# A graph layer on one core: three banks for tiles' products, batch sums in one go, evictions in turn

## The chip, the core and the metric

The kernel runs on one core of a Trainium2 chip. A core has a matrix engine (TensorE, PE in the profile; its weight loads are shown as PEld), a vector engine (VectorE, DVE), a scalar engine (ScalarE, ACT), GpSimd (POOL) and a sync engine (SP) that issues transfers. Each engine runs its own list of instructions in order and waits on semaphores for the others. TensorE writes its products to PSUM, which has eight banks of 2 KiB per partition here, and VectorE and ScalarE read them from there. The metric is the time of one execution on the device in microseconds (us), lower is better. The time before is 18,458.98 us, the median of three runs (18,452.1 to 18,463.75).

## What is computed

Two layers of a relational graph network over 50,000 nodes with 128 features, 850,000 edges sorted by destination and 16 relations, then a residual and a layer norm. Cut to its core:

```python
def _rgcn_layer(h, src, dst, rel, basis, w_comp, loop_w, bias):
    W = jnp.einsum('rb,bio->rio', w_comp, basis)          # 16 relations from 8 bases
    seg = dst.astype(jnp.int32) * N_REL + rel.astype(jnp.int32)
    agg = jax.ops.segment_sum(h[src], seg, num_segments=N_ENT * N_REL)
    agg = agg.reshape(N_ENT, N_REL, -1)
    msg = jnp.einsum('nri,rio->no', agg, W)
    out = msg + h @ loop_w + bias
    return jax.nn.relu(out)

h = _rgcn_layer(x, src, dst, rel_type, basis1, w_comp1, loop_w1, bias1)
h = _rgcn_layer(h, src, dst, rel_type, basis2, w_comp2, loop_w2, bias2)
x = _layernorm(x + h, axis=-1)
```

Everything is float32.

## The kernel before

**Chunks and tiles.** 50,000 of the edges lead from a node to itself and are treated apart (below). The other 800,000 are cut into 625 chunks of ten tiles of 128 edges, and every layer goes over all 625 (`for c in range(C)`, inside `for n, of in enumerate((x, H1))`), 1,250 chunks in all. A tile's edges reach few nodes, 12 at most (`WN`), so a tile is summed into 12 slots, for each of 8 bases.

**Gathers.** For each tile GpSimd issues one indirect transfer (`gather`, L202) that fetches the 128 source rows into `rows[buffer][:, k, :]`. There are five buffers of ten tiles; chunk c+2's gathers are written in the program at chunk c, and a gather waits until the matmul that last read its place is done.

**Tiles' products.** VectorE makes for each chunk a matrix `hot` (`hot_of`, L869 and L876) that holds, for each edge, its weight for each of the 8 bases at the slot of its destination. TensorE multiplies each tile's rows with its part of `hot` (L974, 128 x 96 out). Five tiles, half a chunk, share one PSUM bank `pa` of the pool `ps_a`, which has two. In the text below "product" is one such matmul; it leaves two records in the trace, as the other matmuls of full size do. When a bank has its five products, ScalarE copies it to `aT` in SBUF (L982). `aT` holds four chunks, one batch: 8 bases x 480 slots.

**Batch sums.** When a batch is complete, `slots_of_batch` (L742) multiplies it with the eight basis matrices, summed over them in one bank `ps` (L746), the only bank of the pool `ps_s`; ScalarE copies that to `by_slot` (L752); TensorE turns it by four transposes into a bank `po` (L756); VectorE spreads it (`spread_out`, L734) over four nodes, and TensorE adds each chunk's slots into its groups of nodes in a bank `pn` (L788, `to_nodes`), with masks `own` by VectorE (L771, `masks_of`) as weights. The last chunks of a layer are summed one by one by `slots` (L720).

**Own products.** The edges from a node to itself are done by groups of 512 nodes in `from_itself` (L673): four transposes (L687) into a bank `po`, copied to `hT`, then for each of four parts two matmuls with the bases (L702), each into a bank `po` of the pool `ps_o`, which has two; VectorE weighs each into `by` (L709) and reduces `by` to `ls` (L717). `finish` adds `ls` to the group's `pn` and, in the second layer, norms it.

**The order.** The engines' lists are written out by hand (`tc.manual_schedule`). Between the products, `beside(t, c, owning, summing)` runs one step of the other work after the chunk's product t = 0 to 9: own products after t = 0, 5 and 7; the batch sums (a generator; every `yield` ends a step) after t = 1, 3, 6 and 9; a group's end after t = 2, 6 and 9; and the node sums after t = 8. A step is all that a generator issues up to its next `yield`. A batch's sums start in the chunk after its last. Before the change, steps 1 to 8 issue one of the eight matmuls each, with the copy to `by_slot` in the eighth; steps 9 and 10 issue two transposes each, and 10 and 11 two spreads each.

**PSUM.** The eight banks are: `fixed` 1, `ps_a` 2, `ps_o` 2, `ps_s` 1, `ps_n` 2. Tiles of a pool take its banks in turn: the first write of a tile waits until the tile that had the bank before has been read.

Of the kernel before, what the change touches and what calls it, by code (L numbers as in the profile page):

```python
# [39 lines left out]
F32 = mybir.dt.float32  # L40
# [7 lines left out]
PSUM = bass.MemoryType.PSUM  # L48
DRAM = bass.MemoryType.DRAM

P = 128
# [15 lines left out]
BANK = 512  # L67
# [15 lines left out]
def tile_rgcn_resnorm(  # L83
# [15 lines left out]
    nc = tc.nc  # L99
    N, D = x.shape  # L100
    NR, NB = w_comp1.shape
# [91 lines left out]
            )  # L193
            EACH.append(each)

    ps_a = ctx.enter_context(tc.tile_pool(name="ps_a", bufs=2, space=PSUM))
    ps_o = ctx.enter_context(tc.tile_pool(name="ps_o", bufs=2, space=PSUM))
    ps_s = ctx.enter_context(tc.tile_pool(name="ps_s", bufs=1, space=PSUM))
    ps_n = ctx.enter_context(tc.tile_pool(name="ps_n", bufs=2, space=PSUM))

    def gather(to, of, idx):
        return nc.gpsimd.indirect_dma_start(  # L202
            out=to, out_offset=None, in_=of, in_offset=bass.IndirectOffsetOnAxis(ap=idx, axis=0)
        )
# [384 lines left out]
    def chunked():  # L589
        with (  # L590
# [5 lines left out]
            def ks(c):  # L596
                return min(K, -(-M // P) - c * K)
# [121 lines left out]

            def slots(c, k, aT, n):  # L720

                ps = ps_s.tile([P, BANK], F32, name="ps")
                for b in range(NB):
                    nc.tensor.matmul(
                        ps[: k * WN, :D], aT[:, b, : k * WN], BASIS[n][:, b, :], start=b == 0, stop=b == NB - 1
                    )
                    yield
                yield spread_out(c, ps[:, :D])

            def spread_out(c, of):  # L730

                k = ks(c) * WN
                st = sb.tile([P, J, D], F32, name="slots", bufs=BATCH)
                nc.vector.tensor_tensor(  # L734
                    st[:k],
                    of[:k, None, :].to_broadcast([k, J, D]),
                    which[:k, c, :, None].to_broadcast([k, J, D]),
                    op=OP.mult,
                )
                return st  # L740

            def slots_of_batch(c, aT, st, n):  # L742

                ps = ps_s.tile([P, BANK], F32, name="ps")
                for b in range(NB):
                    nc.tensor.matmul(  # L746
                        ps[:, : BATCH * S], BASIS[n][:, b, :], aT[:, b, :], start=b == 0, stop=b == NB - 1
                    )
                    if b < NB - 1:
                        yield  # L750
                by_slot = sb.tile([P, BATCH * S], F32, name="by_slot", bufs=1)
                nc.scalar.copy(by_slot, ps[:, : BATCH * S])  # L752
                yield
                po = ps_o.tile([P, BANK], F32, name="po")
                for q in range(BATCH):
                    nc.tensor.transpose(po[:S, q * P : (q + 1) * P], by_slot[:, q * S : (q + 1) * S], ident)  # L756
                    if q == 1:
                        yield
                for q in range(BATCH):
                    st[c + q] = spread_out(c + q, po[:, q * P : (q + 1) * P])  # L760
                    if q == 1:
                        yield
                yield
# [57 lines left out]
            def done(steps):  # L821
                for _ in steps:
                    pass
# [38 lines left out]
            for n, of in enumerate((x, H1)):  # L862
# [4 lines left out]
                def hot_of(c, pm):  # L867
                    own = hp.tile([P, K, WN], BF16, name="own")
                    nc.vector.tensor_tensor(  # L869
                        own[:, : ks(c)],  # L870
                        grid[:, None, :].to_broadcast([P, ks(c), WN]),
                        key[:, c * K : c * K + ks(c), None].to_broadcast([P, ks(c), WN]),
                        op=OP.is_equal,
                    )
                    hot = hp.tile([P, K, NB, WN], F32, name="hot", bufs=3)
                    nc.vector.tensor_tensor(  # L876
                        hot[:, : ks(c)],
                        pm[:, c % Q * K : c % Q * K + ks(c), :, None].to_broadcast([P, ks(c), NB, WN]),
                        own[:, : ks(c), None, :].to_broadcast([P, ks(c), NB, WN]),
                        op=OP.mult,  # L880
                    )
                    return hot

                def sum_up(c):
                    at = c % BATCH * S
                    for st[c] in slots(c, ks(c), aTs[c // BATCH][:, :, at : at + S], n):
                        yield
# [52 lines left out]
                for c in range(C):  # L940
                    now[0] = c
                    if n == 0 and c:

                        next(coming, None)
                        while ready[0] + 1 < len(ROWS) and 2 * min(C, c + FETCH + 5) > ROWS[ready[0] + 1]:
                            next(coming)
                    for to in range(0 if c == 0 else c + FETCH, min(C, c + FETCH + 1)):
                        buffer = (n * C + to) % GATHERS
                        for k in range(ks(to)):
                            gather(rows[buffer][:, k, :], of, src[:, to * K + k : to * K + k + 1])  # L950
                    g = rows[(n * C + c) % GATHERS]
                    if c == 0:
                        pm = next(weigh)
                        hots[0] = hot_of(0, pm)
                        hots[1] = hot_of(1, pm)
                        if n == 0:
                            done(first_runs)
                    hot = hots.pop(c)
                    if c % BATCH == 0:
                        aTs[c // BATCH] = hp.tile([P, NB, BATCH * S], F32, name="aT")  # L960
                    aT, place_of = aTs[c // BATCH], c % BATCH * S
                    if c >= ALONE + 2:
                        if c == ALONE + 2:
                            done(summing)
                        summing = sum_up(c - 2)
                    elif c % BATCH == 0:
                        summing = slots_of_batch(c - BATCH, aTs[c // BATCH - 1], st, n) if c else iter(())
                    for k in range(0, K, PER):
                        m = min(PER, ks(c) - k)
                        if m > 0:  # L970
                            pa = ps_a.tile([P, BANK], F32, name="pa")
                        for i in range(PER):
                            if i < m:
                                nc.tensor.matmul(  # L974
                                    pa[:, i * NB * WN : (i + 1) * NB * WN],
                                    g[:, k + i, :],
                                    hot[:, k + i].rearrange("e b w -> e (b w)"),
                                    start=True,
                                    stop=True,
                                )  # L980
                            if i == m - 1:
                                nc.scalar.copy(  # L982
                                    aT[:, :, place_of + k * WN : place_of + (k + m) * WN].rearrange(
                                        "d b (i w) -> d i b w", w=WN
                                    ),
                                    pa[:, : m * NB * WN].rearrange("d (i b w) -> d i b w", i=m, w=WN),
                                )
                            beside(k + i, c, owning, summing)
                    if c + 2 < C:
                        if (c + 2) % Q == 0:  # L990
                            pm = next(weigh)
                        hots[c + 2] = hot_of(c + 2, pm)
                        if c + 3 < C and (c + 3) % Q == 0:
                            weigh = weights(c + 3, n)
                            next(weigh)
                    for one in added_in(c + 1) if c + 1 < C else ():
                        masks[one] = masks_of(one)
                    if n == 0 and c == 3:
                        beginning.close()
                    if n == 0 and c == C - 1:  # L1000
                        done(coming)
                        count_up(pr)
# [10 lines left out]
    def summed():  # L1013
        L1 = dram.tile([N, D], F32, name="L1")
        L2 = dram.tile([N, D], F32, name="L2")
        with tc.tile_pool(name="io", bufs=2) as io, tc.tile_pool(name="sbf", bufs=2) as sb:
# [140 lines left out]
            nodes(L2, norm, also=x)  # L1157

    chunked()
    wrong = nc.values_load(bad[0:1, 0:1], min_val=0, max_val=1)  # L1160
    with tc.If(wrong > 0):
# [40 lines left out]
```

## Time and profile before

| | |
|---|---|
| median of three runs | 18,458.98 us |
| profiled execution | 18,435.78 us, span 18,434.0 us |
| mean granted TensorE clock | 0.762 |
| gathers | 12,500, of 64 KB each (0.95 us of GpSimd) |
| tiles' products L974 | 12,500, in 2,500 banks |
| copies `aT` <- `pa` by ScalarE | 2,500, 0.558 us each |
| matmuls of batch sums L746 | 2,480, in 310 batches |
| own products L702 | 1,568 |

The profile is of one execution. Busy time is shown by engine; a group of instructions is named by its line, engine, operation and by what it writes and reads (`pa<-hot,g`). In a list of instructions, brackets give the engine's idle time before one, and what ended it; "issue" there means that nothing the profile shows ended it, and "remote" that a semaphore did whose source was not found. TensorE's ends are modelled, so the idle times before its instructions are good to some tenths of a microsecond. Groups of TensorE have two records for one instruction, as said above, except the transposes.

### The profile page before, as it was taken

To read this page: it belongs to the slowest core of one execution; us is meant where nothing else is said; L and a number is where in the kernel's file an instruction comes from. 1 tells how busy PE (TensorE), PEld (TensorE's weight loads), DVE (VectorE), ACT (ScalarE), POOL (GpSimd) and SP (SyncE) were. 2 spreads that over 40 slices of the span, in tenths; PEclk is the share of its full clock that TensorE was granted. 3 is DMA by queue.
4 is the path that set the end of the run, shared out by engine and by line. 5 is a ranking of instruction groups with operands and counts; after the bars stand their busy time and mean duration, and the time that the engine had idled before them with its cause. 6 is when DMAs were issued, how large, how long until landed. Compare 5 with 4: busy or idle time off the path is not lost. (4 is left out here: it accounts for less than half of the span.)

```text
span 18434.0 us, 136664 instructions
## 1 busy us (share of the span) xinstructions
PE 11416.0 (62%) x45072; PEld 7482.7 (41%) x45072; DVE 6704.1 (36%) x11496; ACT 1926.2 (10%) x3706; POOL 11894.1 (65%) x12533
## 2 busy tenths in 40 slices
PE   4565555656566666666656666666666666666666
PEld 3343333434344444444444444444444444444444
DVE  4344344444333333333333333333333333333333
ACT  0010000101000000010101111111111111111111
POOL 5666666666666666666656666666666666666665
PEclk8777777777777777777777777777777777777777
DMA  2222222222122122221212222222222222222221
GB/s 70 62 60 58 56 58 60 61 59 60 53 54 55 54 54 54 54 54 54 55 49 57 57 57 57 57 57 57 57 57 58 57 57 57 57 57 57 57 57 51
DMA packets 540034, 1044.31 MB, mean 57 GB/s; under 512 B 214689, under 2 KB 259011, under 8 KB 539319
## 3 DMA queue, kind: packets, MB, share of 16 engines
q0 software_dynamic: 403552, 826.82, 17.1%
q1 hardware_dynamic: 132551, 207.21, 3.5%
q8 instruction: 364, 5.96, 0.1%
q14 instruction: 351, 2.88, 0.0%
q10 hardware_dynamic: 3216, 1.45, 0.0%
HBM read 962.30 MB, written 72.31 MB: 56 GB/s over the span
## 5 line engine op out<-in xcount | busy, mean ns | idle before, releaser
L202 POOL DMA_INDIRECT g<-H,src x6250 | 5929.8, 949 | 3090.0 <-issue 1304.3
L202 POOL DMA_INDIRECT g<-in_x_dram,src x6250 | 5938.3, 950 | 3029.0 <-issue 1267.5
L974 PEld LDWEIGHTS pa<-hot,g 128*128 128x128 f32 x25000 | 4547.2, 229 | 6044.9 <-issue 5010.2
L974 PE MATMUL pa<-hot,g 128*128 128x96 f32 x25000 | 4581.9, 308 | 3009.5 <-issue 2081.6
L746 PE MATMUL ps<-aT,basis 128*128 128x480 f32 x4960 | 2910.5, 672 | 707.7 <-ACT aT L982 476.2
L982 ACT COPY aT<-pa 128x480 f32<-128x480 f32 x2500 | 1388.0, 558 | 15113.3 <-remote 8194.1
L788 PE MATMUL pn<-slots,own 120*128 120x512 f32 x4128 | 2553.4, 741 | 615.4 <-DVE slots L734 289.2
L702 PE MATMUL po<-basis,hT 128*128 128x512 f32 x3136 | 2048.6, 741 | 1319.1 <-DVE by L709 1101.2
L709 DVE TENSOR_TENSOR by<-po,lw 128x512 f32<-128x512 f32 x1568 | 1069.5, 687 | 4167.5 <-remote 1469.1
L876 DVE TENSOR_TENSOR hot<-fixed,own 128x960 f32<-128x960 f32 x1250 | 1447.1, 1158 | 2091.2 <-remote 1580.7
L734 DVE TENSOR_TENSOR slots<-po,which 120x512 f32<-120x512 f32 x1240 | 782.6, 683 | 2747.6 <-remote 933.8
L717 DVE TENSOR_REDUCE ls<-by 128x128 f32<-128x1152 f32 (+1 forms) x784 | 1664.2, 2123 | 34.1
L788 PEld LDWEIGHTS pn<-slots,own 120*128 120x128 f32 x4128 | 865.5, 238 | 1202.2 <-issue 687.4
L746 PEld LDWEIGHTS ps<-aT,basis 128*128 128x128 f32 x4960 | 879.1, 221 | 754.3 <-ACT aT L982 494.9
L702 PEld LDWEIGHTS po<-basis,hT 128*128 128x128 f32 x3136 | 563.8, 225 | 1390.6 <-DVE by L709 1151.7
L869 DVE TENSOR_TENSOR own<-fixed,key 128x120 bf16<-128x120 f32 x1250 | 344.5, 276 | 2106.3 <-remote 1040.9
L756 PE MATMUL po<-ident,by_slot 128*120 128x128 f32 x1240 | 317.9, 348 | 1129.2 <-ACT by_slot L752 742.8
L756 PEld LDWEIGHTS po<-ident,by_slot 128*120 128x120 f32 x1240 | 178.3, 181 | 1171.5 <-ACT by_slot L752 770.4
L771 DVE TENSOR_SCALAR own<-col,node 120x128 f32<-120x128 f32 x2064 | 529.4, 296 | 10.4 <-PE pn L788 10.4
L629 PE MATMUL fixed<-each,is_rel 128*128 128x64 f32 x3140 | 457.2, 300 | 8.4 <-DVE is_rel L624 6.1
L629 PEld LDWEIGHTS fixed<-each,is_rel 128*128 128x128 f32 x3140 | 444.1, 221 | 9.4 <-DVE is_rel L624 7.3
L798 PEld LDWEIGHTS pn<-loop,hT 128*128 128x128 f32 x1568 | 234.5, 213 | 134.0 <-issue 133.6
(137 smaller groups left out, 2892.7 us busy)
## 6 DMA issues: line engine op xcount, KB each, us to landing
g<-in_x_dram,src POOLq DMA_INDIRECT x6250
g<-H,src POOLq DMA_INDIRECT x6250
rel<-REL SPq DMA_DIRECT2D x312, 80.0 KB
h_own<-in_x_dram SPq DMA_DIRECT2D x97, 256.0 KB
xw<-in_x_dram SPq DMA_DIRECT2D x97, 256.0 KB
H<-ls SPq DMA_DIRECT2D x97, 256.0 KB
h_own<-H SPq DMA_DIRECT2D x97, 256.0 KB
out_dram<-ls SPq DMA_DIRECT2D x97, 256.0 KB
```

What stands on the lines that cost most here:

```text
L202: return nc.gpsimd.indirect_dma_start(out=to, out_offset=None, in_=of, in_offset=bass.IndirectOffsetOnAxis(ap=idx, axis=0))
L629: nc.tensor.matmul(of[:, :, j * NB : (j + 1) * NB], is_rel[:m, j * P : (j + 1) * P], EACH[n][:m], start=True, stop=True,)
L702: nc.tensor.matmul(hb[:m], hT[:, j, :m], BASIS[n][:, b : b + few, :].rearrange("p b d -> p (b d)"), start=True, stop=True,)
L709: nc.vector.tensor_tensor(by[:m, b : b + few, :], hb[:m].rearrange("p (b d) -> p b d", d=D), lw[:m, j, g % T, b : b + few, None].to_broadc ...
L717: nc.vector.tensor_reduce(ls[:m, j, :], by[:m].rearrange("p b d -> p d b"), AX.X, OP.add)
L734: nc.vector.tensor_tensor(st[:k], of[:k, None, :].to_broadcast([k, J, D]), which[:k, c, :, None].to_broadcast([k, J, D]), op=OP.mult,)
L746: nc.tensor.matmul(ps[:, : BATCH * S], BASIS[n][:, b, :], aT[:, b, :], start=b == 0, stop=b == NB - 1)
L771: nc.vector.tensor_scalar(own[:k], col4[:k], node4[:k, c : c + 1], float(-g * GN), op0=OP.subtract, op1=OP.is_equal)
L788: nc.tensor.matmul(sums[g], own, of[:k].rearrange("s j d -> s (j d)"), start=c == first(g), stop=c == final(g),)
L876: nc.vector.tensor_tensor(hot[:, : ks(c)], pm[:, c % Q * K : c % Q * K + ks(c), :, None].to_broadcast([P, ks(c), NB, WN]), own[:, : ks(c), ...
L974: nc.tensor.matmul(pa[:, i * NB * WN : (i + 1) * NB * WN], g[:, k + i, :], hot[:, k + i].rearrange("e b w -> e (b w)"), start=True, stop=True,
L982: nc.scalar.copy(aT[:, :, place_of + k * WN : place_of + (k + m) * WN].rearrange("d b (i w) -> d i b w", w=WN), pa[:, : m * NB * WN].rearr ...
```

## The change

`ps_s` is gone, and its bank is the third of `ps_a`. The batch sums take a tile of `ps_o`. Steps 1 and 2 of a batch issue nothing; step 3 (after t = 6 of the batch's first chunk) issues all eight matmuls and the copy to `by_slot`; steps 4 to 8 issue nothing; the transposes stay in steps 9 and 10. In `slots`, all eight steps are empty and the eight matmuls come in one go at the end. Of a chunk's two copies to `aT`, the first (`k == 0`) stays with ScalarE and the second goes to VectorE.

```diff
-    ps_a = ctx.enter_context(tc.tile_pool(name="ps_a", bufs=2, space=PSUM))
+    ps_a = ctx.enter_context(tc.tile_pool(name="ps_a", bufs=3, space=PSUM))
     ps_o = ctx.enter_context(tc.tile_pool(name="ps_o", bufs=2, space=PSUM))
-    ps_s = ctx.enter_context(tc.tile_pool(name="ps_s", bufs=1, space=PSUM))
     ps_n = ctx.enter_context(tc.tile_pool(name="ps_n", bufs=2, space=PSUM))
...
             def slots(c, k, aT, n):
 
-                ps = ps_s.tile([P, BANK], F32, name="ps")
+                for _ in range(NB):
+                    yield
+                ps = ps_o.tile([P, BANK], F32, name="po")
                 for b in range(NB):
                     nc.tensor.matmul(
                         ps[: k * WN, :D], aT[:, b, : k * WN], BASIS[n][:, b, :], start=b == 0, stop=b == NB - 1
                     )
-                    yield
                 yield spread_out(c, ps[:, :D])
...
             def slots_of_batch(c, aT, st, n):
 
-                ps = ps_s.tile([P, BANK], F32, name="ps")
+                for _ in range(2):
+                    yield
+                ps = ps_o.tile([P, BANK], F32, name="po")
                 for b in range(NB):
                     nc.tensor.matmul(
                         ps[:, : BATCH * S], BASIS[n][:, b, :], aT[:, b, :], start=b == 0, stop=b == NB - 1
                     )
-                    if b < NB - 1:
-                        yield
                 by_slot = sb.tile([P, BATCH * S], F32, name="by_slot", bufs=1)
                 nc.scalar.copy(by_slot, ps[:, : BATCH * S])
-                yield
+                for _ in range(NB - 2):
+                    yield
                 po = ps_o.tile([P, BANK], F32, name="po")
...
                             if i == m - 1:
-                                nc.scalar.copy(
+                                (nc.scalar.copy if k == 0 else nc.vector.tensor_copy)(
                                     aT[:, :, place_of + k * WN : place_of + (k + m) * WN].rearrange(
```

Line numbers move by one or two: L702 becomes L701, L746 becomes L748, L756 becomes L757, L974 becomes L975 and L982 becomes L983.

## The prediction

> **What bounds the kernel now.** I read the page first for the share of each engine, then the waits of TensorE and of GpSimd, then one stretch of the timeline, then the rows of tiles `aT` and `by_slot`. The page:
>
> ```profile
> span 18434.0 us, 136664 instructions
> PE 11416.0 (62%) x45072; PEld 7482.7 (41%) x45072; DVE 6704.1 (36%) x11496; ACT 1926.2 (10%) x3706; POOL 11894.1 (65%) x12533
> ```
>
> No engine is full. GpSimd comes nearest to a limit: a gather takes 0.95 us and the next starts 0.30 us later (timeline below), so 12,500 gathers cannot take less than 12,500 x 1.25 = 15,625 us. With 47 us before the first gather and some 60 us after the last that is a floor of 15,730 us. The time above it is GpSimd waiting, and its waits name TensorE, which has not yet given a gathered buffer back. So TensorE's order of work sets the time. It is busy 11,416 us, and what it waits for is in its own waits (total us, times, longest):
>
> ```profile
> PE pa L974 <- issue: 2081.6, 524, 31.3
> PE po L702 <- DVE by L709: 1101.2, 258, 28.7
> PE pa L974 <- ACT aT L982: 833.2, 135, 54.4
> PE po L756 <- ACT by_slot L752: 742.8, 120, 50.5
> PE ps L746 <- ACT aT L982: 476.2, 91, 26.8
> PE po L756 <- issue: 351.5, 106, 13.4
> PE pn L788 <- DVE slots L734: 289.2, 73, 12.6
> PE ps L746 <- issue: 224.2, 130, 14.3
> PE pn L788 <- DVE own L771: 180.9, 55, 24.3
> PE po L702 <- issue: 150.4, 67, 10.7
> ```
>
> "issue" stands where the view found no releaser; the rows show that those waits end just after the same eviction as the named ones, so I add them by tile: products' bank `pa` 2081.6 + 833.2 = 2,915 us in 659 waits; own products `po` 1,252 us in 325; transposes behind `by_slot` 1,094 us in 226; batch sums behind `aT` 700 us in 221; node sums `pn` with their "issue" line (142.1) 612 us. One such wait:
>
> ```profile
> 14002.63 0.69 PE L974 MATMUL pa<-hot,g 128*128 128x96 f32 x4 [0.51 <-ACT sd L579]
> ...
> 14008.04 0.36 PE L974 MATMUL pa<-hot,g 128*128 128x96 f32 x2
> ...
> 14008.23 1.00 PE L746 MATMUL ps<-aT,basis 128*128 128x480 f32 x2
> ...
> 14012.57 0.95 POOL L202 DMA_INDIRECT g<-H,src  x1 [0.30 <-issue]
> 14013.23 0.56 ACT L982 COPY aT<-pa 128x480 f32<-128x480 f32 x1 [8.64 <-remote]
> ...
> 14013.84 1.17 PE L974 MATMUL pa<-hot,g 128*128 128x96 f32 x4 [4.61 <-issue]
> ```
>
> TensorE filled both `pa` banks by 14008.4 and stood until the copy ended at 14013.79. ScalarE was free, and the fifth product of the tile copied had ended at 14005.61: the copy began 7.6 us late. Over the 2,500 copies, row by row, start of copy minus recorded end of the fifth product is 3.2 us at the median, 5.15 in the mean, 12.8 at the ninth tenth. So it is not slow copies (0.56 us) but a late notice of TensorE's progress that costs, and TensorE pays wherever only two buffers lie between it and the engine that must notice. I can't name what delays the notice.
>
> **Third bank for tiles' products.** TensorE may now run one more tile before it needs the late copy: 11,416 / 2,500 = 4.57 us of its work. I could pair 503 of the waits (2,747 us) with a copy; in every one the copy one tile earlier had ended before TensorE stopped, so the third bank frees the start. Cutting each wait by at most 4.57 us, wait by wait, gives -1,613. Bounds: -2,915 (all go) and 0 (the lateness grows by the tile gained).
>
> The page "TensorE: Matmul & The Clock Gate" of the Trainium skill, section "HAM oscillation — how this bites in real kernels", speaks against it: there, double-buffering of PSUM gave no further gain. Its case waited for DMA, this trace's waits end with evictions. By the page this term would be 0.
>
> There is a second reading under which this term is 0: the engine still computed from 14008 to 14013, behind its records. Against it: four records of L974 (two products) took 0.69 us at 14002.63, and the four that begin at 14013.84 took 1.17, at little over half the speed, so the engine had stood still. The same page, section "Part 1: The HAM clock gate", says that the clock halves after an idle window of about 3.4 us, which agrees.
>
> **Batch sums in one go, transposes later.** `by_slot` is copied at the third step of a batch instead of the eighth and transposed at the ninth as before: six steps, 15 products or one and a half chunks (1.5 x 18,434 / 1,250 = 22 us), lie between them instead of two products. The copy starts 4.7 us after the last product in the mean, 11.0 at the ninth tenth (rows of `by_slot`): nearly all is covered. -1,050, bounds -1,094 and -500. The first sum now comes two steps, five products, after the last copy into `aT`; the same stretch takes 2.9 to 3.6 us in the middle half of the batches. 221 waits of 3.2 us in the mean, many short: -450, bounds -700 and 0. The eight sums themselves cost the same (about 0.86 us each, 480 columns twice); they hold up products for 7 us, which gathers 60 us ahead (median, issue of a gather to the product that uses it) and the third bank cover. Without that cover it is 310 x 7 = 2,170 us.
>
> **The sums' bank is taken from own products.** This adds 310 tiles to a rotation of two banks that has about 2,100. By the order of the changed kernel the second `po` tile after the sums, which needs `by_slot` copied, comes 7 or fewer products later in 82 of 300 batches, 14 later in some 80, otherwise further. Release takes 4.7 + 0.56 = 5.3 us; 7 instructions take about 2.3 us. 82 x 3.0 + 80 x 1.5 = +370. Bounds 0 and 310 x 5.3 = +1,640.
>
> **VectorE evicts every second tile.** Nearest row: 512 columns from PSUM in 0.687 us (L709), so 480 in 0.65; ScalarE's 0.56 is the lower end. 1,250 x 0.65 = 812 us of an engine at 36%: hidden as busy time. It shows where TensorE waits for `by`: 325 x 0.65 = +211, bounds 0 and +800. The new wait matters more: VectorE stops at each chunk's end until it sees the chunk's last product, and behind the copy stand `own` (0.28), `hot` (1.16), masks (0.3 each) and the next chunk's `by`. `hot` is made two chunks ahead, 29 us, and is covered; masks have most of a chunk. `by` of the next chunk's first step is needed at its third: +300, bounds 0 and +1,670 (rival below). ScalarE sheds 700 us, worth nothing at 10% busy. No DMA is added or moved; the SP queue keeps its order.
>
> **Where the stalls go.** 1,613 + 1,050 + 450 = 3,113 us are freed, but the notice stays late. Sites left as they are (L702 and L788) are 1,568 + 2,064 = 3,632, or 1.45 a tile, and 325 + 199 = 524 of them wait today, 14%; over the two tiles until TensorE is caught up a freed stretch meets such a wait with 2 x 1.45 x 0.14 = 40%. I let 40% come back: 0.6 x 3,113 = 1,868. Sum: -1,868 + 370 + 211 + 300 = -987. 18,434 - 987 = 17,447. Profiled time 18,435.8 stands 23 us under the median of the runs, 18,459, so I forecast 17,470 us.
>
> **Rivals.**
> - All the way to the gathers. If nothing comes back and the bank costs nothing, 18,434 - 3,113 = 15,320, under the floor of 15,730, so GpSimd would bound it; half-way from the forecast is about 16,500. For it: fewer stalls also mean fewer half-speed stretches (mean granted clock 0.76). Against: every small wait would have to go. 13%.
> - The stalls only move. Nearly all comes back at `po` and `pn`, since the lateness is the same everywhere: 18,434 - 0.3 x 3,113 + 881 = 18,380, or 18,400 as a median. For it: the longest waits are as long at `po` as at `pa`. Against: those two sites wait seldom. 17%, of which 3 within 0.2% and 3 above it.
> - Slower: own products become the bound. VectorE's copy comes 5.15 us after the chunk's last product; with 0.65 + 0.28 + 1.16 + 0.5 the next `by` starts 7.7 us after it. TensorE, running free, reaches the third own step after 7 products and two loads, about 4.5 us: 3.2 us of new wait in each of 1,568 / 3 = 523 chunks = 1,670, and with 220 of the sums' banks in its way 220 x 3.0 = 660. 18,434 - 1,868 + 1,670 + 660 = 18,896, 18,920 as a median. It decides once VectorE's view of the last product is over some 4.5 us late in most chunks with own work. For it: `po` <- `by` is already the second wait. Against: in half the tiles the notice is under 3.2 us late. 30%.
> - The change does all it says: the order shows eight sums in a row and three banks, so I give no chance to the contrary.
>
> **How the numbers follow.** Forecast 40% (16,900 to 18,000), gathers 13%, moved stalls 17%, slower 30%. A measurement of this kernel tells about 0.2% (37 us) from no change. Faster: 40 + 13 + 11 of the moved stalls = 64%; same 3%; slower 30 + 3 = 33%. The range leaves out the last tenth on each side: 16,500 to 18,950.
>
> **What would show it.** Right: TensorE's wait of `pa` for an eviction falls under 1,500 us, `po` <- `by_slot` under 150, batch sums behind `aT` under 350; `po` <- `by` and the new wait of `po` for `by_slot`'s copy rise by no more than 900 together; GpSimd's waits shrink by the same total. Wrong if `po` L701 <- `by` passes 3,000 us (the slower rival), or if the lag from a fifth product to its copy grows by four or more us (the stalls only moved).

## The result and the profile after

The changed kernel takes 18,566.52 us (median of five runs, 18,546.93 to 18,571.6); the kernel before, run beside it, 18,463.75 (18,452.1 to 18,479.11). The ratio is 1.0053 with a 95% interval of 1.0042 to 1.0063: slower by half a per cent. The forecast, 17,470, had the wrong sign; the time lies in the range. The profiled execution's span is 18,568.5 us, at a mean granted clock of 0.758 (0.762 before).

The page of the changed kernel, busy time by engine:

```profile
span 18568.5 us, 135597 instructions
PE 11579.7 (62%) x45072; PEld 7509.3 (40%) x45072; DVE 7468.0 (40%) x12746; ACT 1263.5 (7%) x2456; POOL 11887.4 (64%) x12533
```

VectorE took over 764 us and ScalarE lost 663, as the edit says. No engine is nearer to full. TensorE's waits in the changed kernel (what it waited for: total us, times, longest):

```profile
PE po L701 <- DVE by L708: 1888.0, 316, 33.7
PE pa L975 <- issue: 944.2, 912, 11.7
PE pn L789 <- DVE slots L734: 738.7, 105, 14.3
PE pn L789 <- DVE own L772: 546.4, 161, 18.5
PE pn L789 <- issue: 520.3, 146, 32.9
PE po L701 <- issue: 297.6, 96, 30.7
PE po L748 <- DVE aT L983: 280.6, 46, 35.7
PE po L748 <- DVE by L708: 222.1, 52, 19.6
PE po L701 <- ACT by_slot L752: 219.7, 40, 10.7
PE po L748 <- issue: 200.7, 60, 24.9
PE po L757 <- issue: 44.5, 27, 7.5
PE pa L975 <- DVE aT L983: 44.2, 7, 12.4
PE pa L975 <- ACT aT L983: 33.2, 13, 14.4
```

Added by line, with all the smaller lines of the same view (the prediction had the larger ones alone), in us:

| TensorE waits at | before | after |
|---|---|---|
| tiles' products, `pa` | 3,007 | 1,107 |
| transposes of `by_slot`, `po` | 1,129 | 83 |
| own products, `po` | 1,318 | 2,735 |
| node sums, `pn` | 614 | 1,839 |
| batch sums | 706 | 782 |
| all lines | 6,998 | 6,966 |

The first two waits, at which the change is made, fell by 1,900 + 1,046 = 2,946 us. The next three rose by 1,417 + 1,225 + 76 = 2,718. In sum TensorE stands still for as long as it did, only elsewhere.

One such place in the timeline of the changed kernel (start, us, engine, line, operation, tiles; in brackets the idle time before and what ended it):

```profile
12004.88 1.05 PE L701 MATMUL po<-basis,hT 128*128 128x512 f32 x2
...
12008.27 0.94 POOL L201 DMA_INDIRECT g<-H,src  x1 [0.30 <-issue]
12008.78 0.24 PE L975 MATMUL pa<-hot,g 128*128 128x96 f32 x1 [0.68 <-DMA g<-H,src]
...
12010.18 0.24 PE L975 MATMUL pa<-hot,g 128*128 128x96 f32 x1 [1.16 <-issue]
...
12011.58 0.24 PE L975 MATMUL pa<-hot,g 128*128 128x96 f32 x1 [1.16 <-issue]
...
12012.27 1.47 PE L975 MATMUL pa<-hot,g 128*128 128x96 f32 x7 [0.45 <-issue]
...
12012.41 0.56 ACT L752 COPY by_slot<-po 128x480 f32<-128x480 f32 x1 [9.80 <-remote]
12012.44 0.69 DVE L708 TENSOR_TENSOR by<-po,lw 128x512 f32<-128x512 f32 x1 [9.75 <-remote]
12012.64 0.94 POOL L201 DMA_INDIRECT g<-H,src  x1 [3.42 <-PE pa L975]
...
12017.48 2.08 PE L789 MATMUL pn<-slots,own 120*128 120x512 f32 x2 [3.75 <-issue]
```

The own product of L701 ended at 12005.93 by its record, the batch sum before it earlier still. ScalarE and VectorE, both idle since 12002.7 at the latest, began to read them at 12012.41 and 12012.44, and GpSimd went on at 12012.64: three engines resumed within 0.23 us, more than 6 us late, in a stretch where GpSimd issued no gather for 3.4 us. The notice of TensorE's progress (the update of a semaphore by which the others see what TensorE has finished) reached all of them together.

TensorE itself stood as well: from 12008.78 to 12012.27 it began only three records, 1.4 us apart, the first two of them inside a tile, where it awaits no bank. Such stops inside tiles are most of what is left at `pa`. They went from 180 us in 187 stops to 823 us in 829, while the waits that end within 0.1 us of the awaited bank's copy went from 2,751 us in 491 to 87 us in 32. Of the 829, 463 stand between the two records of one product, and 97% end while an eviction is over 1 us late.

Late notices and pauses of GpSimd often go together. In the second layer GpSimd pauses for 15% of the time, before and after (idle stretches between gathers of over 0.5 us). Of the evictions into `aT` that began over 1 us late although their engine was free, 50% of 636 began in those pauses before the change, and 46% of 584 after it. Per unit of time a late notice is some five to six times as likely to come through while GpSimd pauses. By itself this doesn't tell cause from effect: these evictions begin some 0.2 us (median) before GpSimd goes on, so the notice that starts the copy also ends the pause. What speaks for the pause as the cause is the kernel apart below, where GpSimd's gathers wait for nothing of TensorE.

The gathers' starts show where the time is fixed. Time of each 1,250 gathers, from the instructions' list, in us:

| | first layer | second layer |
|---|---|---|
| before | 1929, 1915, 1882, 1794, 1841 | 1792, 1793, 1793, 1800, 1789 |
| after | 1978, 1955, 1898, 1797, 1846 | 1792, 1797, 1796, 1798, 1798 |

In the second layer the kernels go at 1.435 and 1.437 us a gather, though one waits at `pa` and the other at `po` and `pn`. Of the 134.5 us between the two profiled spans, 48.6 + 39.7 + 15.9 = 104 us lie in the first three stretches, where VectorE also prepares the tables and is busiest.

Numbers further down can't be understood without this: in one group of runs the kernel before took 15,802 us instead of the 18,456 to 18,612 of all others, with the same instructions, and its cause isn't known.

### The profile page after: what moved, and what is told of

The parts are those of the page before. It is cut to its first block, busy times and chain, and to the rows that moved or that the text cites. A ratio compares the mean times of both kernels' runs of the same rounds, so it can differ in the third digit from the quotient of the medians.

```text
span 18568.5 us, 135597 instructions
## 1 busy us (share of the span) xinstructions
PE 11579.7 (62%) x45072; PEld 7509.3 (40%) x45072; DVE 7468.0 (40%) x12746; ACT 1263.5 (7%) x2456; POOL 11887.4 (64%) x12533
## 3 DMA queue, kind: packets, MB, share of 16 engines
q0 software_dynamic: 403552, 826.82, 17.0%
q10 hardware_dynamic: 3216, 1.45, 0.0%
## 5 line engine op out<-in xcount | busy, mean ns | idle before, releaser
L975 PEld LDWEIGHTS pa<-hot,g 128*128 128x128 f32 x25000 | 4102.0, 222 | 3025.7 <-issue 2841.3
L975 PE MATMUL pa<-hot,g 128*128 128x96 f32 x25000 | 4171.8, 301 | 1111.7 <-issue 944.2
L789 PE MATMUL pn<-slots,own 120*128 120x512 f32 x4128 | 2841.4, 815 | 1840.0 <-DVE slots L734 738.7
L701 PE MATMUL po<-basis,hT 128*128 128x512 f32 x3136 | 2159.3, 777 | 2737.2 <-DVE by L708 1888.0
L983 DVE COPY aT<-pa 128x480 f32<-128x480 f32 x1250 | 817.9, 654 | 6714.6 <-PE pa L975 3241.7
L748 PE MATMUL po<-aT,basis 128*128 128x480 f32 x4960 | 2321.5, 626 | 782.0 <-DVE aT L983 280.6
L748 PEld LDWEIGHTS po<-aT,basis 128*128 128x128 f32 x4960 | 1018.9, 211 | 1887.3 <-issue 1304.3
L701 PEld LDWEIGHTS po<-basis,hT 128*128 128x128 f32 x3136 | 580.3, 231 | 2864.6 <-DVE by L708 1952.9
L983 ACT COPY aT<-pa 128x480 f32<-128x480 f32 x1250 | 698.3, 559 | 10631.3 <-remote 6138.0
L752 ACT COPY by_slot<-po 128x480 f32<-128x480 f32 x310 | 173.4, 559 | 3539.0 <-remote 1643.4
L661 PE MATMUL po<-each,lrel 64*128 64x32 f32 (+1 forms) x800 | 198.9, 408 | 232.3 <-DVE lrel L654 137.2
```

The lines of the kernel that those rows point to most:

```text
L701: nc.tensor.matmul(hb[:m], hT[:, j, :m], BASIS[n][:, b : b + few, :].rearrange("p b d -> p (b d)"), start=True, stop=True,)
L748: nc.tensor.matmul(ps[:, : BATCH * S], BASIS[n][:, b, :], aT[:, b, :], start=b == 0, stop=b == NB - 1)
L789: nc.tensor.matmul(sums[g], own, of[:k].rearrange("s j d -> s (j d)"), start=c == first(g), stop=c == final(g),)
L975: nc.tensor.matmul(pa[:, i * NB * WN : (i + 1) * NB * WN], g[:, k + i, :], hot[:, k + i].rearrange("e b w -> e (b w)"), start=True, stop=True,
L983: (nc.scalar.copy if k == 0 else nc.vector.tensor_copy)(aT[:, :, place_of + k * WN : place_of + (k + m) * WN].rearrange("d b (i w) -> d i ...
```

## The experiments

Each group ran on one chip, beside the kernel before; a ratio is to that kernel. "Lag" is the start of an `aT` copy less the recorded end of its fifth product, mean of 2,500: 5.15 us before, 4.80 after. A variant that is given with neither a range nor a ratio ran once.

**Half the gathers.** Left out: every second gather; the odd tile's products use the even tile's rows.

```diff
-                        for k in range(ks(to)):
+                        for k in range(0, ks(to), 2):
...
-                                    g[:, k + i, :],
+                                    g[:, (k + i) // 2 * 2, :],
```

> The kernel before with every second gather left out; the products of an odd tile use the rows of the even tile before it. TensorE, VectorE and ScalarE do the same work as before. Theory A (TensorE's own work, behind its records, sets 14.35 us a chunk in the second layer): the time stays within 3% of 18,459. Theory B (the gathers set the pace: GpSimd at work delays the notice of TensorE's progress): the time falls by 3,000 us or more, and the copy of a bank starts under 1 us after its fifth product at the median. Theory C (stalls on a notice that is late for a reason apart from the gathers): GpSimd has no waits left to lose, the time stays within 5%, and the lag stays near 5 us in the mean.

10,786.7 us (18,573.6 before, beside it), TensorE 89% busy, lag 0.72. With all of its own work and two buffers of `pa`, TensorE waits at `pa` 117.0 + 81.5 = 198 us by the two lines that made up 2,915 before. So the lateness belongs to the gathers, not to the number of banks.

**No own products.** Left out: L702, its products in `by` and the reduction, so `ls` gets the bias alone.

```diff
                 for j in range(J):
+                    yield
+                    nc.vector.tensor_copy(ls[:m, j, :], by[:m, NB, :])
+                    yield
...
-                    for b in range(0, NB, few):
```

> The kernel before without the own products: the 1,568 matmuls L702, VectorE's by and its reduction are left out, ls is set to the bias. TensorE loses 1,350 to 2,050 us of recorded work and 1,250 us of waits, VectorE 2,700 us. Theory A: the second layer's chunk goes from 14.35 us to under 13 us. Theory B: the chunk of the second layer stays at 14.2 us or above, and only the first layer may gain. Theory C: TensorE loses a place where it stalls, so the time falls by 1,000 us or more in both layers.

18,413.8 us (18,573.6 beside it), although TensorE lost 1,167 us of work and VectorE 2,558. The second layer goes at 1.44 us a gather, as theory B had it; TensorE's wait of `pa` rose to 2,793 + 1,185 us. Work taken from TensorE turns into waiting as well.

**The evictions, apart.** act_both: the changed kernel with both copies on ScalarE; dve_turn: the kernel before with the copies in turn.

```diff
-                                (nc.scalar.copy if k == 0 else nc.vector.tensor_copy)(
+                                nc.scalar.copy(
```

> The changed kernel with both evictions of a chunk by ScalarE again; three banks and sums in one go stay. If VectorE's evictions cost what was lost, in the first layer where VectorE also prepares rows: 18,400 to 18,470. If the sums in the own products' banks cost it: 18,560 as the changed kernel. If the third bank is worth 1,600 us once VectorE is out of the way: under 17,500.

> The kernel before with only the evictions in turn (two banks, sums as before). If VectorE's evictions cost the loss of the change: 18,560 or more, with the loss in the first layer and the second layer's chunk still at 14.35 us. If turns help the late notice: below 18,400.

act_both 18,567.1, ratio 0.9995 (0.9985 to 1.0004); dve_turn 18,605.0, ratio 1.0018 (1.0009 to 1.0028). The ranges that were expected are for a chip on which the kernel before takes 18,459; here it takes 18,573.6, so the ratios decide. The third bank and the sums in one go change nothing, and the change without VectorE's copies loses nothing. Added to the kernel before, VectorE's copies cost a third of the loss, less than expected; the other two thirds would come only where they meet the other edits. The changed kernel itself wasn't run in this group, so these shares set the ratios of two groups side by side.

**Few rows.** 8 of 128 rows in each gather; the other rows hold zeros.

```diff
-gather(rows[buffer][:, k, :], of, src[:, to * K + k : to * K + k + 1])
+gather(rows[buffer][:8, k, :], of, src[:8, to * K + k : to * K + k + 1])
```

> The kernel before, but each of the 12,500 gathers fetches 8 rows in place of 128 (the other 120 rows of a tile are zeros). GpSimd's instructions and waits stay, the transfers shrink to a sixteenth. Theory R (the rows in transfer delay the notice of TensorE's progress): the lag from a bank's fifth product to its copy falls under 1 us at the mean and the time to what GpSimd needs, at most 15,900, less if a short gather also issues faster. Theories I (GpSimd's issuing) and W (its waits on TensorE's semaphore, one a gather, for each of which TensorE posts): if an instruction still takes 1.25 us, the time stays above 18,000 and the lag near 5 us.

18,614.5 us (18,604.9 beside it), 1.447 us a gather, lag 5.10. A sixteenth of the rows, no gain: bytes aren't the cause. The packets on GpSimd's queue are as many as before (403,552, with 59 MB in place of 827), so their number isn't ruled out by this run.

**Gathers that nothing reads.** apart: gathers go to buffers that nothing reads, the products read zeros. iotas: each gather is a GpSimd iota of 1,024 numbers. loads: each gather is a plain load of 128 rows by SP's queue. All three have three buffers of rows, filled with zeros once, and in all three nothing of the graph is computed.

```diff
+    unread = [consts.tile([P, K, D], F32, name=f"u{i}") for i in range(2)]
...
-gather(rows[buffer][:, k, :], of, src[:, to * K + k : to * K + k + 1])
+gather(unread[to % 2][:, k, :], of, src[:, to * K + k : to * K + k + 1])
```

> The kernel before with all 12,500 gathers going to two buffers that nothing reads; the products read three buffers of zeros. GpSimd issues and moves as much as before, but hardly waits for TensorE (37 waits in place of 12,487), and TensorE posts 7,368 times in place of 19,957. Theory W: notices are prompt, lag under 1 us in the mean, time at the gathers' floor, about 15,800. Theories I and R: while the gathers run (they are free to run to the end of each layer, 7,850 us a layer), lag stays near 5 us or grows, TensorE gets less than 1,250 tiles' banks done in 7,850 us of them, and the time is over 17,000.

> The kernel with unread gathers, with each of the 12,500 gathers replaced by a GpSimd iota of 1,024 numbers (about 1 us by the rows of the smaller ones), no transfer. GpSimd is busy about 12,500 us if it runs without a break. If any work of GpSimd holds TensorE's notices back: TensorE again gets 500 to 600 records in 1,500 us while they run, and the time is over 20,000. If it takes the issue of indirect transfers, or what their landing does: notices are prompt, 10,300 to 12,600 us.

> The kernel with unread gathers, with each of the 12,500 gathers replaced by a plain load of 128 rows of x on the SP queue: as many bytes and landings, GpSimd nearly idle. If the landings of transfers hold TensorE's notices back: TensorE gets 500 to 600 records in 1,500 us while they run, time over 20,000. If it takes GpSimd's issue: notices prompt, time 10,300 to 13,000, bounded by TensorE or by the SP queue, which has 12,500 more issues.

25,912.5, 13,204.1 and 10,031.9 us; the last two lie outside the ranges expected, above and below. Stretches of apart (window, its length, then busy us and instructions of TensorE, its weight loads, VectorE, ScalarE, GpSimd; granted clock, DMA share, GB/s):

```profile
9000.00:10500.00 1500.00, 199.55 (x532) 120.26 (x532) 65.61 (x99) 21.34 (x39) 1160.34 (x1072) 0.53 0.18 48
15000.00:16500.00 1500.00, 191.92 (x514) 116.48 (x514) 67.39 (x115) 23.31 (x46) 1165.84 (x1073) 0.53 0.18 49
22500.00:24000.00 1500.00, 1424.90 (x6870) 958.13 (x6868) 958.58 (x1659) 307.85 (x618) 0.00 (x0) 0.96 0.07 20
```

While GpSimd issues gathers freely, TensorE gets through 514 to 532 records in 1,500 us; once they are over, through 6,870. The lag is 64 us in the mean from 7,500 to 10,500 us and 65 us from 13,500 to 21,000, and 0.36 us after 22,500. No gather here writes what a product reads, and GpSimd's waits on TensorE fell from 12,487 to 37, so it is neither the data nor those waits. The same view of iotas:

```profile
7500.00:9000.00 1500.00, 1402.61 (x6698) 937.77 (x6698) 1029.39 (x1635) 299.27 (x602) 1412.18 (x1428) 0.96 0.06 20
```

GpSimd is 94% busy and TensorE runs at full pace (lag 0.21), so it isn't GpSimd at work as such. In loads the rows land by another queue; lag 0.20, and TensorE is nearly full. The page of loads:

```profile
PE 9379.4 (94%) x45072; PEld 6312.9 (63%) x45072; DVE 6662.1 (66%) x11499; ACT 1936.6 (19%) x3706; POOL 25.1 (0%) x33
```

What is left is the issue of indirect gathers by GpSimd, with what its queue does for them. A plain load issued by GpSimd wasn't run, so whether it takes an indirect transfer or any transfer of GpSimd's stays open.

**Last tile first.** A chunk's gathers are issued from its last tile to its first, which takes most of GpSimd's waits on TensorE away (12,487 to 1,282), before and after the change.

```diff
-                        for k in range(ks(to)):
+                        for k in reversed(range(ks(to))):
```

> The kernel before with a chunk's ten gathers issued last tile first. The first then waits for the last product of the chunk that had the buffer, and the other nine need no wait: GpSimd waits for TensorE 1,282 times in place of 12,487 and TensorE posts 9,550 times in place of 19,957. All else is the same. Theory W: the time falls to between 15,750 and 16,500, lag under 1 us in the mean. Theories I and R: between 18,300 and 19,500, slower rather than faster because a buffer is given back a chunk at a time.

> The changed kernel with the same order of gathers. Theory W: 15,750 to 16,500, and if TensorE is then what bounds it, the third bank shows and it is faster than the kernel before with that order. Theories I and R: as the changed kernel, 18,500 to 19,500.

19,081.1, ratio 1.026 (1.0243 to 1.0277), and 18,966.4, ratio 1.0193 (1.0176 to 1.021). The lag stays at 5.33 and 4.51 us: fewer waits of GpSimd on TensorE don't make the notices earlier. With this order the change gains 115 us, the only pair in which it gains anything, and the second layer goes at 1.506 and 1.485 us a gather.

**Three buffers.** `GATHERS = 3` instead of 5, before and after the change.

> The kernel before with three buffers of rows in place of five, so GpSimd can issue 30 gathers ahead and not 50 before it has to wait for TensorE. If what counts is that GpSimd stops often enough for notices to come through, and a stretch of gathers without a wait holds them back: 17,000 to 18,300. If the share of time in which GpSimd stands is what TensorE needs however it is cut: 18,400 to 18,700. If the lead hides something: slower, 18,700 to 20,000.

> The changed kernel with three buffers of rows. Same cases as above; if notices come through more evenly the third bank of products should now tell: 500 us or more under the kernel before with three buffers. If the gathers still set the pace: within 1% of that kernel.

18,324.4, ratio 0.9841 (0.9824 to 0.9857), and 18,364.5, ratio 0.9866 (0.9849 to 0.9882): by their ratios both beat both kernels. 18,324 lies between the ranges expected. The lag of three is 5.02 us. Its profile has 1,838 to 1,847 us for each of the first layer's first three stretches, where before has 1,882 to 1,929 (on another chip); its second layer isn't faster (1,806 to 1,812). The change on top of it costs 40 us.

**Spaced, two buffers, ScalarE.** three_act: the changed kernel, three buffers, ScalarE's copies. spaced: three with an iota of 32 numbers behind each gather. two: before with two buffers, gathers issued one chunk ahead.

```diff
 gather(rows[buffer][:, k, :], of, src[:, to * K + k : to * K + k + 1])
+nc.gpsimd.iota(spacer, pattern=[[1, 32]], base=0, channel_multiplier=0, allow_small_or_imprecise_dtypes=True)
```

> The changed kernel with three gather buffers and both of a chunk's evictions on ScalarE. Theory (VectorE's evictions are the change's only cost, the buffers a gain beside it): 18,364.5 less the 100 us that act_both won, about 18,270 us, that is 0.981 of before and a little under three's 18,324. Rival (the gain of fewer buffers already holds what act_both won, since both lie in the first layer): 18,320 to 18,370.

> three with a GpSimd iota of 32 numbers (some 0.16 us by the rows of the longer ones) behind every gather, so that a gather can follow the one before in no less than about 1.45 us instead of 1.25. Theory A (notices are held back while gathers follow one another without a gap): lag from fifth product to copy falls from 5.0 us to under 2.5, and GpSimd's waits on TensorE with it; the time is then set by 12,500 x 1.45 = 18,125 plus the ends, 18,150 to 18,350. Theory B (each gather holds the notices by a fixed amount, whatever lies between): lag stays 4 to 6 us, and the added work comes on top in part or in full, 18,400 to 20,000 us.

> Before with two gather buffers and gathers issued one chunk ahead. If what helps in three is that GpSimd runs less far ahead: as fast as three in the first layer, 18,250 to 18,350 us. Rival (a chunk's gathers then wait for products that ended only one chunk ago, so the loop from notice to gather to product is too short to hide its latency): second layer's pace above 1.434 us a gather, 18,600 us or more.

This is the group beside which the kernel before took 15,802.4 us (15,793.8 to 15,806.3, 19 runs). three_act 15,802.0, ratio 1.0001 (0.9991 to 1.001); two 15,813.7, ratio 1.0008 (0.9999 to 1.0018); spaced 16,604.3, ratio 1.0508 (1.049 to 1.0525). Notices were prompt here in the kernels that were profiled: lag 0.155, 0.10 and 0.09. TensorE's waits in three_act:

```profile
PE pa L975 <- DMA g<-H,src: 1446.2, 2119, 5.3
PE pa L975 <- DMA g<-in_x_dram,src: 1445.0, 2021, 24.7
PE pa L975 <- ACT aT L983: 105.7, 160, 1.0
PE po L701 <- DVE by L708: 68.2, 57, 3.4
```

It waits for rows to land and for hardly anything else: GpSimd issues every 1.25 us, and 12,500 of them set the time. The three tests are therefore inconclusive about late notices, since there were none to remove. They show what the kernel does without them: 15,802 to 15,814 with two, three or five buffers, and 15,802 with the third bank. In spaced the iota took 0.18 us, but the step from gather to gather grew by only 0.064 us in the mean (1.258 to 1.323, against three_act), which times 12,500 is the 802 us that it costs.

**The change with prompt notices.** The loads layout again: the changed kernel (after_loads, in the group with 15,802), then in one group the kernel before (loads_again) and the changed one with ScalarE's copies (after_loads_act). Nothing of the graph is computed.

> The changed kernel with every gather replaced by a plain load by the SP queue into a buffer that nothing reads, as in loads (10,031.9 us); the products read zeros, so nothing of the graph is computed. Theory (the third bank has something to remove only while TensorE's notices are late): in loads TensorE waited for pa's eviction only 37 us and for the transposes behind by_slot 49 us, so the change has nothing left to take: 9,950 to 10,150 us, pa wait under 40, and po behind by rises from 304 by no more than 200. Rival (the bank and the moved sums are worth something of their own, or cost something of their own): under 9,950, or above 10,150.

> The same kernel as loads (before with plain loads in place of the gathers, products of zeros), taken again because after_loads ran on another chip than loads. If the layout runs alike on every chip: 9,950 to 10,110 us, and after_loads' 11,291.7 is then the change's doing. If the chip makes the difference: 11,000 us or more here too, or a time far from 10,032.

> after_loads with both of a chunk's evictions on ScalarE: the third bank and the moved sums alone, while notices are prompt. Theory (VectorE's evictions are the change's cost: in after_loads VectorE stood 2,764 us at aT for TensorE's last product, and by and slots came late behind it): 9,900 to 10,200 us, beside loads_again within 1.5%. Rival (the sums in one go or the own products' bank cost as well): 10,400 us or more, with TensorE's wait po behind by over 500.

11,291.7, 10,041.4 and 10,376.9 us; the kernel before took 18,456.5 beside the last two. loads_again repeats loads within 0.1%, so I compare across groups in this layout. The change without VectorE's copies costs 335 us, and these copies 915 more. TensorE's waits in after_loads:

```profile
PE po L704 <- DVE by L711: 622.7, 335, 6.8
PE pn L792 <- DVE slots L737: 310.0, 147, 8.2
PE po L751 <- DVE by L711: 131.0, 89, 5.1
PE po L751 <- DVE aT L986: 113.6, 65, 2.7
```

and what VectorE itself waits for there:

```profile
DVE aT L986 <- PE pa L978: 2763.9, 721, 13.0
DVE by L711 <- PE po L704: 736.1, 330, 7.9
```

VectorE stands 2,764 us at the chunk's end for TensorE's last product, and `by` and `slots` come late behind it; in loads TensorE waits 304 and 51 us for these two, and for the eviction of `pa` 37 us in all. My theory had 9,900 to 10,200 for after_loads_act and missed; its `po` behind `by` is 433 + 87 = 520 us, as the rival had it, with 10,377 just under the rival's 10,400. The sums in the own products' bank cost something too. Where notices are prompt, the third bank has nothing to remove.

## Why the prediction was wrong

**The step that failed** is the reading "So TensorE's order of work sets the time", and with it the rule of "Where the stalls go" that 40% of the freed time comes back. All of it came back. In no_own TensorE has a tenth less work and the time falls by 0.9%; in half_gathers it has all of its work, in the same order, and the time falls by 42%. GpSimd does wait because buffers aren't given back, but what is late is the notice, and its lateness isn't tied to a place in TensorE's list. It belongs to GpSimd's gathers (lag 5.15 us with them, 0.20 with loads by SP). The second layer goes at 1.43 to 1.45 us a gather in before, after, act_both, no_own, few_rows and three: with or without the third bank, with a tenth of TensorE's work taken out, with a sixteenth of the rows. Why the pace is the same is a reading only: if late notices come through mostly in GpSimd's pauses, and GpSimd pauses only when it has run out of buffers, such a loop settles at one pace whatever TensorE does between. It fits these six kernels; with the gathers in another order the pace is another (1.506 and 1.485). spaced, made to test it, met prompt notices, so it isn't shown.

**Third bank** (-1,613). `pa` fell by 1,900 us, near the forecast by luck: the waits for a bank fell by 2,664 us (2,751 to 87), close to the bound of -2,915, and 643 us of stops inside tiles, which the prediction didn't have, came in at the same line. As time it is 0 (act_both, ratio 0.9995). The page "TensorE: Matmul & The Clock Gate" of the Trainium skill, section "HAM oscillation — how this bites in real kernels", found no further gain in double-buffering PSUM, and I set it aside because its case waited for DMA. The ratio of act_both agrees with its outcome. That half_gathers nearly empties this wait with two banks shows that the banks weren't the limit.

**Batch sums in one go** (-1,050 and -450). The transposes' wait fell by 1,046. Batch sums: 706 to 782, not -450; 222 us of it is now the wait for a bank that own products hold (`po` L748 behind `by`).

**The sums' bank** (+370) shows as 220 us of `po` L701 behind `by_slot` and those 222, inside its bounds.

**VectorE evicts** (+211 and +300). The waits that come from VectorE rose by far more: own products behind `by` from 1,252 to 2,186 us with the "issue" line, and all of `pn` by 1,225. The prediction put masks aside since they "have most of a chunk"; they stand in VectorE's list behind a copy that waits for a late notice, and `pn` behind `own` went from 181 to 546. As time, act_both gives the whole loss to these copies, and dve_turn a third of it.

**The floor** of 15,730 us held: 15,802 was measured where notices were prompt, and there the rows' landing is all that TensorE waits for.

**The rivals.** "The stalls only move" is what happened, at the sites named. Its price, 18,380, still let 30% of the freed time stay freed; at 0% and with the bank's and VectorE's 881 it is 19,315, too slow: added waits seem to be absorbed just as freed ones are. Its test failed too: the lag was to grow by four us or more, and it fell from 5.15 to 4.80. The slower rival's limit (`po` behind `by` over 3,000) wasn't reached; its mechanism shows once notices are prompt, in after_loads. Of the signs under "What would show it", `pa` under 1,500 and the transposes under 150 came true while the time rose. Batch sums behind `aT` (281 + 201 = 481 us against 350) and the rise of `po` (934 + 220 = 1,154 against 900) missed theirs. The sign that counted was that GpSimd's waits shrink, and they grew: time between gathers beyond 1.25 us from 2,710 to 2,843 in sum.

**A slip.** Half-way between the forecast and the floor is 16,600 and not 16,500, which moves the range's lower end a little and decides nothing.

## What to carry to other kernels

When a wait ends late because of a late notice, one more buffer can empty that wait and gain nothing, as the lateness shows up at the next place; before pricing waits one by one, find what the slowest loop is made of, by leaving out half of it, as half_gathers does. When time freed at one site is to be credited, the test is whether the engine that sets the pace (here GpSimd, gather by gather) would start earlier. A copy that is moved to another engine brings its wait along, and all that stands behind it in that engine's list.

## What the hardware showed unexpectedly

While GpSimd issues indirect gathers back to back, other engines learn of TensorE's progress late: lag 5.15 us in the mean, against 0.20 with plain loads of as many rows and 0.21 with GpSimd busy on iotas; with gathers running freely in apart the lag is 64 to 65 us, and TensorE falls to 514 records in 1,500 us, a thirteenth of its pace. TensorE is held up itself too, inside tiles, where no bank is awaited: 823 us in the changed kernel and 1,373 in act_both, and none with plain loads. Notices from ScalarE and VectorE weren't late: TensorE began within 0.1 us of the copy's end in 491 of 519 waits for ScalarE's copies before, and in 284 of 297 for VectorE's in dve_turn. It doesn't always happen: in one group of runs, with the same gathers every 1.25 us, the lag was 0.09 to 0.16 us, and the kernel before ran in 15,802 us, 14% to 15% less than in the others, one of which was on a chip with the same number. Which outside condition decides this, by what way the issue of gathers holds TensorE's notices back, and why fewer buffers help only in the first layer, stays open.
